# Two-layer convolution block on one core: scattered evictions in every group, sums on VectorE, separate result tiles at the end of the 7x7 stage

## The chip, the core and the metric

The kernel runs on one core of a Trainium2 chip. The metric is the device time of one execution in microseconds; the median of several runs is compared. TensorE (PE) multiplies, VectorE (DVE), ScalarE (ACT) and GpSimd (POOL) do the rest, and SyncE (SP), ACT and POOL issue transfers to 16 DMA engines. All data are 32-bit floats.

## What is computed

The input x has 384 channels of 192 x 192 pixels. Layer 0 normalises over groups of 12 channels, projects to q, k and v, takes the maximum over 2 x 2 pixels, runs a 3 x 3 depthwise convolution, forms channel attention in 8 heads with four top-k softmaxes, and adds the projected result to x. Layer 1, which the change touches, is a depthwise 7 x 7 convolution with residual:

```python
w_sym = (weight + rot90(weight, 1) + rot90(weight, 2) + rot90(weight, 3)) * 0.25
x = x + dwconv(groupnorm(x), w_sym, stride=1, pad=3)     # 384 channels, 7 x 7 each
```

## The kernel before

Layer 0 fills the first 2100 us or so and isn't touched. It leaves the new x in device memory as `sd`, cut into an 8 x 8 raster of pixels (64 partitions, each with a coarse image), and the 7 x 7 filters as matrices in `wt`.

The 7x7 stage turns each channel into matmuls. The contraction runs over the pixels of a window and over some marker rows for the borders (126 partitions); the output is 128 partitions, which are places within 8 x 8 cells and row halves, by 288 columns (6 tiles of 24 cells, two strips each). The loop `for n in range(steps)` has 48 steps of `CB` = 8 channels. Each step works in four quarters, `q` = 0 to 3, of two channels: 16 matmuls into one PSUM tile `pc` (there are four, of two banks each), then one eviction into `apart`, which multiplies by the reciprocal deviation `rb` of the channel. Two steps make a group of `CO` = 16 channels, so there are 24 groups (numbers 0 to 23) and one `apart` tile for each.

Around the matmuls these things happen:

- **Loads, two steps ahead.** `load_w` (line 1702, on SP) brings the weights `w` into one of three buffers. `load_main` (line 1711, on POOL) brings the pixels `mains` into 64 partitions of one of three buffers.
- **Copies.** `below` fills the other partitions of `mains` from those that were loaded. POOL copies one part (lines 1864 and 1868), ACT another, each in two instructions. On ACT the first copy follows the eviction of q = 0 and the second that of q = 1.
- **Sums into the weights.** `middle(n + 1)` (line 1769) adds the diagonal for the residual, from `mids`, to the weights of the next step, four channels per instruction. From step 1 on it runs on POOL, after POOL's copies.
- **Evictions.** ACT takes q = 0, 1 and 2 (line 1981), DVE q = 3 (line 1979). In all groups but the last they write rows of 48 elements. In the last group (`dense`) the matmul reads its columns in another order, and the eviction writes single elements 32 words apart, so that what a transpose reads lies together.
- **Transposes.** `swapped` (line 1914) turns 32 x 32 blocks of `apart` into rows of the image in a tile `res`, in six instructions per group. It is a generator: the loop calls it once after each eviction, so group g's transposes run in the two steps after the group. There are two `res` buffers.
- **Stores.** `stored` (line 1889) writes a group with eight transfers on SP. They are put into SP's queue at the start of the second step after the transposes began, behind that step's weight load. For group 22 they are issued after its last transpose. For group 23 they are issued after every second transpose, half on SP and half on ACT.

`keep` holds an instruction at its place in the order in which the program is written. Each engine works in order, and so does each queue: a weight load on SP behind eight stores is issued after them.

Of the kernel before, what the change touches and what calls it, by code (L numbers as in the profile page):

```python
# [8 lines left out]
F32 = mybir.dt.float32  # L9
# [4 lines left out]
P = 128  # L14
# [4 lines left out]
HW = 192  # L19
# [40 lines left out]
TR = 32  # L60
NT = HW // TR
ED = 8
NJ = HW // ED
JP = NJ + 1
STRIPS = NT * JP
PITCH = 160
# [5 lines left out]
Q = 32  # L72
RQ = Q // ED
WIN = 2 * ED
GP = 3 * ED - 3
ONE = (WIN - 1) * ED
ROWS = 6
# [13 lines left out]
CO = 16  # L91
# [4 lines left out]
def conv_preact_d2(  # L96
# [17 lines left out]
    nc = tc.nc  # L114
# [198 lines left out]
    keep = tc.keep_in_program_order  # L313
    with tc.tile_pool(name="stp", bufs=1) as stp, tc.tile_pool(name="xsp", bufs=5) as xsp:
# [77 lines left out]
        mids = stp.tile([P, KT + 1], F32, name="mids0")  # L392
# [4 lines left out]
        for b in reversed(range(NB)):  # L397
            if b == NX - 1:
# [7 lines left out]
                for k, i in ((0, 0), (1, 1), (KT, 2)):  # L406
                    ps = total(f"gs_mid0_{k}", 1, terms[i])
# [56 lines left out]
        for b in [*range(NB - 2, NX, -2), NX, *reversed(range(NX))]:  # L464
            n = 2 if b > NX else 1
# [19 lines left out]
        ps = total("gs0_2", 2, [(sel(1, 2), ds[1]), (shared[:, P:], de), (whole, d)])  # L485
# [124 lines left out]
    with ExitStack() as bx:  # L610
# [269 lines left out]
        begun_dw, ready = {}, []  # L880
# [739 lines left out]
    with ExitStack() as ex_:  # L1620
# [135 lines left out]

        half = (ED + 1) * RQ

        def middle(n, add):

            centre = ws[n].rearrange("p b c n -> p b (c n)")
            for i in range(0, CB, 4):
                g = (n * CB + i) // GC
                mid = bass.AP(
                    ws[n].tensor, ws[n].offset + i * ED * ED,
                    [[ws[n].ap[0][0], 3 * Q], [CB * ED * ED + RQ, 2], [ED, 4 * ED], [1, RQ]],
                )
                keep(
                    add(  # L1769
                        mid, mid,  # L1770
                        mids[0 : 3 * Q, g].unsqueeze(2).to_broadcast([3 * Q, 2, 4, ED * RQ]),
                        ALU.add,
                    )
                )
# [33 lines left out]
        along(sb, std1, 0)()  # L1808
        busy(idle[:, 0], 5)
        middles(0)  # L1810
        middle(0, nc.vector.tensor_tensor)
        sumw = const.tile([P, KT], F32, name="sumw")
        with tc.issue_after(settled):
            nc.vector.tensor_reduce(sumw, w7s.rearrange("p t a b -> p t (a b)"), AX.X, ALU.add)
# [64 lines left out]
            for _ in copying:  # L1879
                pass  # L1880

        def stored(n, res, lo=0, hi=NT, queues=(nc.sync,)):

            for i, quad in enumerate((0, 2, 1, 3)):
                h, g = divmod(quad, 2)
                for k in range(2):
                    row = TURNS[h][k] * ED + (1 - g) * RQ + lo * TR
                    keep(
                        queues[i % len(queues)].dma_start(
                            bass.AP(  # L1890
                                out.tensor, out.offset + (n * CO * HW + row) * HW,
                                [[HW * HW, CO], [TR * HW, hi - lo], [1, RQ * HW]],
                            ),
                            res[quad * Q + k : (quad + 1) * Q : 2, lo:hi].rearrange(
                                "p t r n -> p t (r n)"
                            ),
                        )
                    )

        columns = 2 * NJ  # L1900

        groups = C // CO
        ready = []

        def swapped(n, apart):

            last = n == groups - 1
            res = outp.tile([P, NT, RQ, HW], F32, name=f"res{n}", tag="res")
            for k in range(NT):
                src = apart[:, k].rearrange("p c (s j) -> p j (c s)", j=NJ)  # L1910
                if last:
                    src = apart[:, k].rearrange("p c n -> p (c n)").rearrange("p (j n) -> p j n", j=NJ)
                keep(
                    nc.vector.transpose(  # L1914
                        res[:, k].rearrange("p r (j q) -> p j r q", q=ED)[:, :, ::-1], src
                    )
                )
                if last and k % 2:
                    stored(n, res, k - 1, k + 1, (nc.sync, nc.scalar))
                yield  # L1920
            if n == groups - 2:
                stored(n, res)
            elif not last:
                ready.append(lambda: stored(n, res))

        for lo, hi, copy in ((0, 2, nc.gpsimd), (2, 5, nc.gpsimd), (5, CB, nc.vector)):
            whole(below(0, copy.tensor_copy, *LOWER[0], slice(lo, hi)))
# [5 lines left out]
        for n in range(steps):  # L1933
# [5 lines left out]
            if n + 1 < steps:  # L1939
                for copy, cs in ((nc.gpsimd, slice(0, CB)),) if n else (  # L1940
                    (nc.gpsimd, slice(0, CB // 2)), (nc.vector, slice(CB // 2, CB))
                ):
                    whole(below(n + 1, copy.tensor_copy, *LOWER[0], cs))
                middle(n + 1, nc.gpsimd.tensor_tensor)
            w, main = ws.pop(n), mains.pop(n)
            if n % 2 == 0:
                apart = outp.tile([P, NT, CO, columns], F32, name=f"apart{n}", tag="apart")
            order = [[JP, NT], [PITCH, 2]]
            dense = n // 2 == groups - 1
            if dense:  # L1950
                order.reverse()
            for q in range(CB // 2):
                ps = pc.tile([P, 2, 512], F32, name=f"pc{n}_{q}", tag="pc")
                for k in range(2):
                    i = 2 * q + k
                    for j in range(2):
                        for h in range(2):
                            keep(
                                nc.tensor.matmul(  # L1959
                                    ps[h * 2 * Q : (h + 1) * 2 * Q, k, 0 : 2 * NT * NJ],  # L1960
                                    w[0 : ONE + ROWS, j, i],
                                    bass.AP(
                                        main.tensor, main.offset + i * RUN + 2 * h * PITCH + j,
                                        [[main.ap[0][0], ONE + ROWS], *order, [1, NJ]],
                                    ),
                                    start=(j == 0), stop=(j == 1), skip_group_check=True,
                                )
                            )
                c = n * CB + 2 * q
                o = n % 2 * CB + 2 * q  # L1970
                src = ps[:, :, 0 : 2 * NT * NJ].rearrange("p k (t n) -> p k t n", t=NT)
                dst = apart[:, :, o : o + 2].rearrange("p t k n -> p k t n")
                if dense:
                    src = ps[:, :, 0 : 2 * NT * NJ].rearrange("p k (s n) -> p k s n", s=2)
                    dst = apart.rearrange("p t c n -> p (t c n)").rearrange(
                        "p (n c s) -> p c s n", c=CO, s=2
                    )[:, o : o + 2]
                if q == 3:
                    keep(nc.vector.tensor_scalar_mul(dst, src, rb[:, c : c + 1]))
                else:  # L1980
                    keep(nc.scalar.mul(dst, src, rb[:, c : c + 1]))  # L1981
                next(swapping, None)
                if q == 0 and n + 1 < steps:
                    lower = below(n + 1, nc.scalar.copy, *LOWER[1])
                next(lower, None)
                if q == 1 and n in later:
                    dgs = [diagonal(v, later[n]) for v in (std1, rstd1)]
            if n in later:
# [69 lines left out]
```

## Time and profile before

| | |
|---|---|
| Time, median of 3 runs | 2581.61 us (2578.67 to 2583.24) |
| Profiled execution | 2587.33 us |
| its span | 2585.6 us |
| granted TensorE clock, mean | 0.976 |
| busy shares of the span: PE, DVE, ACT, POOL | 91%, 81%, 51%, 51% |
| 7x7 stage, first to last matmul | 2117.1 to 2556.4 us |
| from last matmul to the end | 29 us |

The profile is one execution; its times count from the start of the span. A row of a group of instructions gives the line in the code, the engine, the operation, what is written and read with its shape, the count, the busy time and mean duration in ns, and after the bar the idle time of the engine just before these instructions with what ended it. A wait for several things is put down to the last that came. A DMA share of 1 means that all 16 DMA engines had a packet in work all the time.

### The profile page before, as it was taken

What the parts mean: (1) busy time and instruction counts of PE and PEld (TensorE: products, weight loads), DVE (VectorE), ACT (ScalarE), POOL (GpSimd) and SP (SyncE); (2) the same over time, 40 slices, a digit from 0 to 9 for tenths busy, and PEclk for the clock granted to TensorE, in tenths of its full rate; (3) what the DMA queues carried; (4) which work ended last, traced back from release to release, by engine and by line L of the source; (5) the groups of instructions that cost most, each with busy time, mean ns of one, the idle gap of its engine ahead of it and who ended that gap; (6) DMA issues with size and microseconds to landing.
All of it is one profiled execution on the core that took longest, in us unless ns stands there. A gap on an engine that the chain in (4) does not pass through costs nothing.

```text
span 2585.6 us, 29955 instructions
## 1 busy us (share of the span) xinstructions
PE 2350.5 (91%) x9655; PEld 1436.8 (56%) x9655; DVE 2098.3 (81%) x2875; ACT 1314.0 (51%) x2424; POOL 1306.6 (51%) x1329
## 2 busy tenths in 40 slices
PE   0298999999999999999989999999999959998995
PEld 0144565555556666665555666666666745565553
DVE  7986688888888887878879999999888958777775
ACT  0031576666667677677521323222322457776774
POOL 1013688888887767766522211211211367767672
PEclk9998999999999999999999999999999979999997
DMA  9995254453553323233343866765764598999997
GB/s 377 404 222 126 71 117 120 106 144 96 118 137 75 97 64 102 58 82 82 80 142 103 240 215 193 259 228 189 245 249 153 207 272 295 334 323 327 331 335 220
DMA packets 439386, 487.14 MB, mean 188 GB/s; under 512 B 291149, under 2 KB 369197, under 8 KB 434749
## 3 DMA queue, kind: packets, MB, share of 16 engines
q1 hardware_dynamic: 407558, 339.17, 43.5%
q0 software_dynamic: 28032, 141.97, 17.1%
q10 hardware_dynamic: 3639, 4.09, 0.6%
q8 instruction: 77, 1.26, 0.2%
q14 instruction: 80, 0.66, 0.1%
HBM read 309.18 MB, written 147.47 MB: 177 GB/s over the span
## 4 chain that ended last, share of the span: by engine, by line
PE 72%; DMA 13%; DVE 9%; ACT 2%; POOL 1%; issue 1%; SPq 1%; ACTq 0%; DVEq 0%; POOLq 0%
PE pv L568 20%; PE bank_b L1040 10%; PE bank_y L1040 7%; PE bank_d L1040 6%; PE bank_c L1040 6%; PE bank_x L1040 6%; PE pc L1959 6%; DMA w<-wt 5%; PE pr L1474 4%; PE po L1450 3%; DVE st L342 3%; DMA out_dram<-res 3%; DMA xs<-in_x_dram 2%; DMA mains<-sd 2%; PE grams L802 2%
## 5 line engine op out<-in xcount | busy, mean ns | idle before, releaser
L568 PE MATMUL pv<-xv,wq 128*128 128x384 f32 x1512 | 495.2, 488 | 10.7 <-DVE rows L574 6.0
L1959 PE MATMUL pc<-mains,w 126*64 126x288 f32 x3072 | 410.8, 420 | 41.1 <-POOL w L1769 25.2
L568 PEld LDWEIGHTS pv<-xv,wq 128*128 128x128 f32 x1512 | 288.5, 191 | 208.8 <-DVE rows L574 6.6
L1541 POOL DMA_DIRECT2D sd<-sx x180 | 135.1, 755 | 529.2 <-DVE sx L1505 517.9
L903 POOL TENSOR_TENSOR qk<-qk,more 128x384 f32<-128x384 f32 x290 | 310.0, 1073 | 142.9 <-ACT more L902 132.8
L1959 PEld LDWEIGHTS pc<-mains,w 126*64 126x64 f32 x3072 | 245.3, 137 | 205.5 <-POOL w L1769 39.6
L1914 DVE STREAM_TRANSPOSE res<-apart 128x768 f32<-128x768 f32 x144 | 282.6, 2011 | 78.1 <-DMA w<-wt 41.3
L601 DVE SCALAR_TENSOR_TENSOR vb<-rows,wd,vb 128x576 f32<-128x576 f32 x360 | 293.6, 817 | 10.7
L903 POOL TENSOR_TENSOR qk<-qk,rows 128x384 f32<-128x384 f32 x216 | 230.2, 1070 | 97.2 <-ACT rows L902 90.2
L935 DVE SCALAR_TENSOR_TENSOR bank_r<-ring,wd,bank_r 128x384 f32<-128x384 f32 x383 | 236.4, 617 | 6.8
L1040 PE MATMUL bank_b<-rows,more 128*128 128x384 f32 x528 | 219.8, 498 | 9.2 <-ACT bank_c L1140 9.0
L1505 DVE TENSOR_TENSOR sx<-xr,y 128x576 f32<-128x576 f32 x180 | 204.1, 1175 | 18.1 <-ACT y L1482 15.2
L1119 DVE TENSOR_TENSOR rows<-bank_c,rows 128x384 f32<-128x384 f32 x132 | 73.2, 554 | 137.9 <-PE bank_c L1040 76.4
L574 DVE TENSOR_REDUCE rows<-pv 128x192 f32<-128x768 f32 x144 | 137.6, 956 | 44.1 <-PE pv L568 44.0
L902 ACT ACTIVATE more<-ring,wd 128x384 f32<-128x384 f32 x290 | 170.3, 609 | 0.0
L1525 ACT ACTIVATE wq<-sx,negmid 128x1152 f32<-128x1152 f32 x96 | 120.6, 1256 | 96.6 <-DVE sx L1505 94.3
L1981 ACT ACTIVATE apart<-pc,rb 128x576 f32<-128x576 f32 x144 | 110.2, 765 | 99.4 <-PE pc L1959 61.3
L1040 PE MATMUL bank_x<-xq,wq 128*128 128x384 f32 x378 | 154.7, 491 | 1.0 <-ACT bank_b L1092 1.0
L1040 PE MATMUL bank_y<-xq,wq 128*128 128x384 f32 x378 | 155.0, 492 | 0.0
L1457 ACT ACTIVATE gl<-po 128x288 f32<-128x288 f32 x96 | 39.5, 411 | 222.5 <-PE po L1450 222.5
L1864 POOL COPY mains<-mains 32x2560 f32<-32x2560 f32 (+3 forms) x49 | 110.0, 2246 | 75.9 <-DMA mains<-sd 74.8
L1474 PE MATMUL pr<-gl,wp 128*128 128x288 f32 x576 | 142.6, 406 | 0.0
(343 smaller groups left out, 4474.4 us busy)
## 6 DMA issues: line engine op xcount, KB each, us to landing
mains<-sd POOLq DMA_DIRECT2D x46, 1312.0 KB, 10.3
out_dram<-res SPq DMA_DIRECT2D x184, 288.0 KB
xr<-in_x_dram SPq DMA_DIRECT2D x45, 1152.0 KB
xq<-in_x_dram SPq DMA_DIRECT2D x21, 2304.0 KB
xv<-in_x_dram SPq DMA_DIRECT2D x126, 384.0 KB
sd<-sx POOLq DMA_DIRECT2D x132, 320.0 KB, 7.8
xs<-in_x_dram SPq DMA_DIRECT2D x24, 1536.0 KB
w<-wt SPq DMA_DIRECT2D x47, 504.0 KB
```

The costliest lines, as they stand in the source:

```text
L568: nc.tensor.matmul(ps[:, u, 0 : RB * HW], wq[:, kt, o : o + P], xb[:, u, kt, :], start=(kt == 0), stop=(kt == KT - 1),)
L574: nc.vector.tensor_reduce(rows[ct][:, 1 + t0 : 1 + t0 + UT, 1 : PS + 1], ps[:, :, 0 : RB * HW].rearrange("p u (a w b) -> p u w a b", a=2, ...
L601: pin(nc.vector.scalar_tensor_tensor(dst, src, w, dst, ALU.mult, ALU.add))
L902: keep(nc.scalar.mul(part.rearrange("p (h w) -> p h w", w=PS), src, w))
L903: keep(nc.gpsimd.tensor_tensor(flat, flat, part, ALU.add))
L935: nc.vector.scalar_tensor_tensor(into, src, w, before, ALU.mult, ALU.add)
L1040: nc.tensor.matmul(ps[:, 0:HN], lhs, rhs, start=start, stop=True, skip_group_check=True)
L1474: nc.tensor.matmul(ps[:, 0:H], wp[:, ct, ot * P : (ot + 1) * P], gl[:, ct, h * H : (h + 1) * H], start=(ct == 0), stop=(ct == KT - 1),)
L1505: nc.vector.tensor_tensor(bass.AP(flat.tensor, flat.offset + 1 + (a * ED + e) * STRIPS, [flat.ap[0], [JP, NT], [1, NJ], [2 * STRIPS, ED // ...
L1541: engine.dma_start(sdv[r + a, cs, RQ - e : ED - e, o : o + n], bass.AP(flat.tensor, flat.offset + 1 + (a * ED + e) * STRIPS - (e > 0), [fl ...
L1914: nc.vector.transpose(res[:, k].rearrange("p r (j q) -> p j r q", q=ED)[:, :, ::-1], src)
L1959: nc.tensor.matmul(ps[h * 2 * Q : (h + 1) * 2 * Q, k, 0 : 2 * NT * NJ], w[0 : ONE + ROWS, j, i], bass.AP(main.tensor, main.offset + i * RU ...
```

## The change

- `middle` always runs on VectorE. In the loop it is called at q = 3, just ahead of the eviction of q = 3, instead of after POOL's copies.
- All groups use the column order and the scattered evictions of the former last group, and all transposes read dense blocks. `apart` is laid out for that.
- Evictions with even q are on ACT and those with odd q on VectorE: two each per step.
- ACT makes both of its copies after the eviction of q = 0.
- `places` names the tiles of a group's results. Groups 0 to 21 have one `res` tile as before. Group 22 has half of a `res` tile and the space of `edges`; group 23 has a third of one `res` tile, the space of `mids`, and a third of another. `edges` and `mids` are no longer needed by then.
- Group 22 is stored in two halves, each as soon as its three transposes are issued; group 23 in three parts, as before on SP and ACT.

```diff
-                middle(n + 1, nc.gpsimd.tensor_tensor)
...
+        def places(n):
+
+            def spare(t, k):
+                flat = bass.AP(t.tensor, t.offset, [t.ap[0], [1, k * RQ * HW]])
+                return flat.rearrange("p (t r n) -> p t r n", t=k, n=HW)
+
+            def own(i):
+                return outp.tile([P, NT, RQ, HW], F32, name=f"res{n}_{i}", tag="res")
+
+            if n < groups - 2:
+                return [own(0)]
+            if n == groups - 2:
+                return [own(0)[:, 0 : NT // 2], spare(edges, NT // 2)]
+            return [own(0)[:, 0:2], spare(mids, 2), own(1)[:, 0:2]]
+
         def swapped(n, apart):
 
-            last = n == groups - 1
-            res = outp.tile([P, NT, RQ, HW], F32, name=f"res{n}", tag="res")
-            for k in range(NT):
-                src = apart[:, k].rearrange("p c (s j) -> p j (c s)", j=NJ)
-                if last:
-                    src = apart[:, k].rearrange("p c n -> p (c n)").rearrange("p (j n) -> p j n", j=NJ)
-                keep(
-                    nc.vector.transpose(
-                        res[:, k].rearrange("p r (j q) -> p j r q", q=ED)[:, :, ::-1], src
+            k = 0
+            for res in places(n):
+                for i in range(res.shape[1]):
+                    keep(
+                        nc.vector.transpose(
+                            res[:, i].rearrange("p r (j q) -> p j r q", q=ED)[:, :, ::-1],
+                            apart[:, k + i],
+                        )
                     )
-                )
-                if last and k % 2:
-                    stored(n, res, k - 1, k + 1, (nc.sync, nc.scalar))
+                    if i + 1 < res.shape[1]:
+                        yield
+                if n < groups - 2:
+                    ready.append(lambda: stored(n, res))
+                else:
+                    stored(n, res, k, (nc.sync, nc.scalar) if n == groups - 1 else (nc.sync,))
                 yield
-            if n == groups - 2:
-                stored(n, res)
-            elif not last:
-                ready.append(lambda: stored(n, res))
+                k += res.shape[1]
...
-                apart = outp.tile([P, NT, CO, columns], F32, name=f"apart{n}", tag="apart")
-            order = [[JP, NT], [PITCH, 2]]
-            dense = n // 2 == groups - 1
-            if dense:
-                order.reverse()
+                apart = outp.tile([P, NT, NJ, 2 * CO], F32, name=f"apart{n}", tag="apart")
...
-                                        [[main.ap[0][0], ONE + ROWS], *order, [1, NJ]],
+                                        [[main.ap[0][0], ONE + ROWS], [PITCH, 2], [JP, NT], [1, NJ]],
...
-                src = ps[:, :, 0 : 2 * NT * NJ].rearrange("p k (t n) -> p k t n", t=NT)
-                dst = apart[:, :, o : o + 2].rearrange("p t k n -> p k t n")
-                if dense:
-                    src = ps[:, :, 0 : 2 * NT * NJ].rearrange("p k (s n) -> p k s n", s=2)
-                    dst = apart.rearrange("p t c n -> p (t c n)").rearrange(
-                        "p (n c s) -> p c s n", c=CO, s=2
-                    )[:, o : o + 2]
-                if q == 3:
+                src = ps[:, :, 0 : 2 * NT * NJ].rearrange("p k (s n) -> p k s n", s=2)
+                dst = apart.rearrange("p t j (c s) -> p c s (t j)", s=2)[:, o : o + 2]
+                if q == 3 and n + 1 < steps:
+                    middle(n + 1)
+                if q % 2:
                     keep(nc.vector.tensor_scalar_mul(dst, src, rb[:, c : c + 1]))
...
                 if q == 0 and n + 1 < steps:
                     lower = below(n + 1, nc.scalar.copy, *LOWER[1])
-                next(lower, None)
+                    next(lower)
+                    next(lower)
```

More of the change, by code (lines that the diff above doesn't have):

```diff
@@ L1757, in conv_preact_d2, with middle @@
         half = (ED + 1) * RQ
-        def middle(n, add):
+        def middle(n):
             centre = ws[n].rearrange("p b c n -> p b (c n)")
@@ L1768, in middle @@
                 keep(
-                    add(
+                    nc.vector.tensor_tensor(
                         mid, mid,
@@ L1810, in conv_preact_d2 @@
         middles(0)
-        middle(0, nc.vector.tensor_tensor)
+        middle(0)
         sumw = const.tile([P, KT], F32, name="sumw")
@@ L1880, in whole, with stored @@
                 pass
-        def stored(n, res, lo=0, hi=NT, queues=(nc.sync,)):
+        def stored(n, res, lo=0, queues=(nc.sync,)):
             for i, quad in enumerate((0, 2, 1, 3)):
@@ L1891, in stored @@
                                 out.tensor, out.offset + (n * CO * HW + row) * HW,
-                                [[HW * HW, CO], [TR * HW, hi - lo], [1, RQ * HW]],
+                                [[HW * HW, CO], [TR * HW, res.shape[1]], [1, RQ * HW]],
                             ),
-                            res[quad * Q + k : (quad + 1) * Q : 2, lo:hi].rearrange(
-                                "p t r n -> p t (r n)"
-                            ),
+                            res[quad * Q + k : (quad + 1) * Q : 2].rearrange("p t r n -> p t (r n)"),
@@ L1897, in stored @@
                         )
                     )
-        columns = 2 * NJ
         groups = C // CO
         ready = []
-        def swapped(n, apart):
-            last = n == groups - 1
-            res = outp.tile([P, NT, RQ, HW], F32, name=f"res{n}", tag="res")
-            for k in range(NT):
-                src = apart[:, k].rearrange("p c (s j) -> p j (c s)", j=NJ)
-                if last:
-                    src = apart[:, k].rearrange("p c n -> p (c n)").rearrange("p (j n) -> p j n", j=NJ)
-                keep(
-                    nc.vector.transpose(
-                        res[:, k].rearrange("p r (j q) -> p j r q", q=ED)[:, :, ::-1], src
-                    )
-                )
-                if last and k % 2:
-                    stored(n, res, k - 1, k + 1, (nc.sync, nc.scalar))
+        def places(n):
[9 more added lines that the diff above has]
+            return [own(0)[:, 0:2], spare(mids, 2), own(1)[:, 0:2]]
```

## The prediction

> **What bounds the kernel now.** All edits lie in the 7x7 stage, so I read first the busy time by stretch: the stage without its start and end (2162 to 2538 us), and the end (2556 to 2586 us). Columns: length; busy time (instructions) of PE, PE weight load, DVE, ACT, POOL; granted clock; DMA share; GB/s.
>
> ```profile
> 2162.00:2538.00 376.00, 350.00 (x2625) 209.54 (x2626) 277.68 (x167) 275.97 (x206) 261.35 (x205) 0.97 0.97 331
> 2386.00:2394.00 8.00, 8.00 (x44) 4.11 (x46) 5.96 (x4) 3.82 (x4) 6.92 (x6) 0.67 0.97 324
> 2266.00:2274.00 8.00, 8.00 (x68) 4.55 (x66) 6.85 (x4) 5.71 (x5) 6.39 (x5) 1.00 0.80 237
> 2556.00:2586.00 30.00, 0.39 (x2) 0.00 (x0) 6.69 (x7) 0.00 (x0) 0.00 (x0) 0.54 0.60 157
> ```
>
> DVE, ACT and POOL work about 70 to 74% of the stage, PE 93%, and the DMA engines 97%. One step (8 channels) moves 504 KB of weights, 1312 KB of pixels and, on average, 1152 KB of results: 3.04 MB, at 331 GB/s 9.2 us. From the timeline, 40 steps (last VectorE eviction at 2170.96 to that at 2538.76) take 367.8 us: 9.2 us each. Undisturbed, a step takes 8.4 us (PE from 2413.26 to 2421.67). So the transfers set the pace. The missing 0.8 us per step comes in lumps: two or three groups run free, then the chain shows this.
>
> ```profile
> 2369.44 15.60 DMA w<-wt
> 2385.08 0.10 issue
> 2385.18 0.73 POOL w L1769
> 2385.95 27.10 PE pc L1959 x193
> ```
>
> Weights issued behind eight stores land late, POOL adds the sums, PE starts 3.6 us late; afterwards its clock is 0.67 for some microseconds, and only then has the DMA a little air (0.75 to 0.88 in such slices). The waits say the same; the columns are total us, times, longest.
>
> ```profile
> DVE res L1914 <- DMA w<-wt: 41.3, 14, 4.4
> DVE res L1914 <- DMA out_dram<-res: 29.5, 7, 11.8
> PE pc L1959 <- POOL w L1769: 25.2, 13, 3.6
> POOL w L1769 <- DMA w<-wt: 12.3, 9, 2.2
> ```
>
> The second part is the end: the last PE matmul is at 2556.4, the span ends at 2585.6. The timeline from the last group's evictions (first two rows, step 46) on:
>
> ```profile
> 2544.81 1.35 ACT L1981 ACTIVATE apart<-pc,rb 128x576 f32<-128x576 f32 x1
> 2548.57 1.20 DVE L1979 TENSOR_SCALAR apart<-pc,rb 128x576 f32<-128x576 f32 x1
> 2557.70 1.84 DVE L1914 STREAM_TRANSPOSE res<-apart 128x768 f32<-128x768 f32 x2
> 2571.31 1.84 DVE L1914 STREAM_TRANSPOSE res<-apart 128x768 f32<-128x768 f32 x2 [11.78 <-DMA out_dram<-res]
> 2577.82 1.84 DVE L1914 STREAM_TRANSPOSE res<-apart 128x768 f32<-128x768 f32 x2 [4.67 <-DMA out_dram<-res]
> ```
>
> The transposes of one tile wait for the stores of its earlier parts: 16.45 us in all, though the data don't meet. The DMA share is 0.60 here.
>
> **The change, part by part.** The last group of before already has the scattered evictions and dense transposes, so their prices stand in the trace. For the rest, the stage's groups:
>
>
> ```profile
> L1914 DVE STREAM_TRANSPOSE res<-apart 128x768 f32<-128x768 f32 x144 | 282.6, 2011 | 78.1 <-DMA w<-wt 41.3 <-DMA out_dram<-res 29.5 <-ACT mains L1864 6.9
> L1981 ACT ACTIVATE apart<-pc,rb 128x576 f32<-128x576 f32 x144 | 110.2, 765 | 99.4 <-PE pc L1959 61.3 <-issue 35.7
> L1979 DVE TENSOR_SCALAR apart<-pc,rb 128x576 f32<-128x576 f32 x48 | 39.3, 819 | 54.6 <-PE pc L1959 54.6
> L1769 POOL TENSOR_TENSOR w<-w,mids 96x256 f32<-96x256 f32 x94 | 66.7, 727 | 15.3 <-DMA w<-wt 12.3
> L1864 POOL COPY mains<-mains 32x1280 f32<-32x1280 f32 x1 | 1.9, 1895 | 1.0 <-DMA mains<-sd 1.0
> ```
>
> *Load per step.* DVE before: 3 transposes x 2.01 + 1 eviction x 0.82 = 6.85 us. After: 3 x 0.92 (1.84 for two, above) + 2 evictions x 1.20 + 2 sums x 0.42 (the two that DVE did before the stage, 415 and 422 ns) = 6.0. ACT: 3 x 0.74 + copies 2.32 + 2.19 = 6.7 before, 2 x 1.31 + 4.51 = 7.1 after. POOL: 0.52 + 2.31 + 2.19 + 2 x 0.73 = 6.5 before, 5.0 after. All stay under the 8.4 us of PE. As busy time this saves DVE about 40 us and POOL 68, and none of it is on the path while the transfers set the pace: it buys nothing by itself. The matmuls only read their columns in another order, as the last group does already at the same speed.
>
> [...]
>
> *ACT order.* ACT now runs eviction q0, then both copies, without q1 between them. The next step's matmuls wait for the copies: 0.74 + 2.32 + 0.74 + 2.20 = 6.0 becomes 1.3 + 2.32 + 2.20 = 5.8. The free step of 8.4 us ends with this chain (PE waits 0.2 us for ACT's copy), so it can fall to about 8.2; and where pixels land late, ACT is 0.7 us quicker. Both are gains of compute that the transfers can take back.
>
> *Sums to DVE.* They stood on POOL behind its copies of the next pixels and ahead of its next pixel DMA; a late weight transfer held that DMA back (issued at 2386.54, where PE was free for it near 2382.3). Now that DMA goes out up to 4 us earlier after a stall. After a late landing PE waits for 2 x 0.42 instead of 2 x 0.73 us: 0.6 us x 8 stalls = 5 us. But on DVE the sums stand behind the eviction q1 and two transposes, and in a group's first step the first transpose waits for the stores of two groups before. Call T the time from the step's start to that transpose. The second sum ends at max(T + 0.95, 4.3) + 1.2 + 1.9 + 0.84, about T + 5.0, or 8.3 if T is under 3.35. From the DVE timeline, T over 21 groups is 0.7 to 7.6, mean 3.5. Where T is largest the weights were later still (10 us and more after the step's start), so the new wait hides behind the old; over the other groups the excess sums to 3 to 4 us of PE. Behind a sum that waits stand eviction q3 and the next transposes; PE needs that PSUM buffer only 6.4 us into the next step, and results leave two steps later, so nothing else is late.
>
> [...] The row agrees that there is contention (POOL's half copy beside DVE's copies took 1895 ns, half of the usual 2310 is 1155). If POOL lost all of 2 x 0.42, its step would be 5.9 us instead of 5.0, still under the 6.5 of before. I take nothing on the path.
>
> Stage, summed: -5 (shorter add) - 5 (ACT order, 30 free steps x 0.18) + 4 (sums behind late stores), about -6 of compute, of which the saturated transfers give half: **-3 us**. Bounds: the DMA share of 0.97 leaves 3% of 376, so -12 at best; +5 if the excess of T counts in full and nothing is gained.
>
> *End.* With own tiles no transpose waits for its neighbours' stores: six of 0.92 from 2557.7, done at 2563.3. Group 22 is now stored in halves, the first in step 46 and the second at about 6.5 us into step 47 (2555), where before all eight stores (2.36 MB) were issued only after the last slow transpose at 2555.6. Group 23's stores, four on SP and four on ACT per pair, at 0.6 to 0.8 us an issue: SP first works off the second half until about 2560, then 12 x 0.7 = 8.4 us, to 2568.5. Each store also waits in the program for a DMA eight issues before it, so a pair follows the landing of the last one, 2.2 to 2.5 us (the last two in the chain of before): three pairs from 2560 end issuing at 2568 as well. Landing 2.5, end 0.9: 2571.5 against 2585.6, **-14 us**. By bytes, 3.5 MB from 2555 at 331 GB/s end at 2566 plus landing, so the DMA doesn't forbid it. Bounds: -16 (issues at 0.6) and -9 (issues at 1.35 us as in the stage, eleven on SP's way). The new third tile takes the buffer of group 22's first half, landed well before 2561: no wait of weight.
>
> **Sum.** -14 - 3 = -17. The profiled execution took 2587.33 us, its span 2585.6 (1.7 around it), so 2570.3 for it; it stands 5.7 above the median of the runs, 2581.61, from which I forecast 2564.6.
>
> **Rivals.**
> (1) *The stage gains as well.* [...] For it: the dips to 0.75 come only after a PE stall. Against it: the stage moves the same bytes, and most slices are full.
> (2) *The end doesn't give what it should.* If the remaining transfers or the issue queues set the end, -9 or less there and +3 in the stage: 2575.6. For it: stores took 1.35 us an issue in the stage. Against it: a share of 0.60 at the end.
> (3) *Slower: the sums wait behind the transposes on DVE.* One mechanism: in each group's first step, stores landing late hold the transpose, the eviction q1 and so the next step's weights. Price: T - 3.35 per group, 21 groups. It decides against the end's 14 us when the mean excess passes 0.67 us, that is T about 4.0 in every group, with nothing given back by the transfers. Ten of 21 groups have T at 4.0 or above now. At T = 4.5 everywhere it costs 24 and the time is 2592. Against it: most of these late groups wait for their weights longer anyway, and a delayed PE issues fewer transfers, which brings T down.
>
> **How the numbers follow.** Forecast 0.60 (own range 2558 to 2573), rival 1 0.17, rival 2 0.13, rival 3 0.10. Single runs of before spread by 0.2%, 5.2 us, which is about what can be told from no change. Faster: 0.60 + 0.17 + half of rival 2 = 0.83; same: the other half and a little of rival 3, 0.08; slower 0.09. The range takes the forecast, rival 1 to -12 and -16, rival 2 to -9 and +5: 2553 to 2578.
>
> **What would show it.** Right: dense transposes near 0.92 us and DVE evictions near 1.20 in every group; the mean step between 8.9 and 9.2 us at a DMA share of 0.96 or more; no transpose after the last matmul waiting for a DMA; last matmul to end about 15 us instead of 29. Wrong: PE waiting mostly for the sums on DVE while weights have landed (rival 3); a step of 8.6 (rival 1); stores after the last matmul that queue behind one another past 20 us (rival 2).

## The result, and the profile after

The changed kernel takes 2594.64 us (median of 16 runs, 2588.39 to 2604.25), the kernel before, run beside it, 2584.64 us (16 runs, 2578.67 to 2599.57). The ratio is 1.0035, with a 95% interval of 1.0021 to 1.0049: slower by 0.35%, some 9 us, where 17 us less were forecast.

The two profiled executions (2587.33 us before, 2597.32 us after) can be cut at the first and the last matmul of the 7x7 stage:

| | before | after | forecast |
|---|---|---|---|
| first to last matmul of the stage | 439.3 us (2117.1 to 2556.4) | 451.7 us (2115.6 to 2567.3) | -3 us |
| last matmul to the end | 29.2 us | 28.2 us | -14 us |

So the stage lost 12.4 us and the end gained 1.0. Both accounts failed, for different reasons. The busy time by stretch of the kernel after, with the columns of the prediction (length; PE, PE weight load, DVE, ACT, POOL busy; clock; DMA share; GB/s):

```profile
2162.00:2538.00 376.00, 335.72 (x2540) 248.09 (x2536) 231.54 (x277) 273.49 (x158) 193.63 (x118) 0.94 0.93 318
2386.00:2394.00 8.00, 7.13 (x34) 3.52 (x36) 4.90 (x4) 2.89 (x3) 4.18 (x2) 0.58 0.99 354
2394.00:2402.00 8.00, 8.00 (x70) 4.57 (x68) 4.98 (x7) 6.33 (x5) 3.45 (x3) 1.00 0.53 156
2562.00:2570.00 8.00, 5.28 (x43) 3.76 (x38) 4.74 (x6) 2.03 (x2) 0.00 (x0) 1.00 0.14 35
2567.00:2595.50 28.50, 0.28 (x2) 0.00 (x0) 6.58 (x7) 0.00 (x0) 0.00 (x0) 0.56 0.59 145
```

VectorE lost 46 us of work and GpSimd 68, about as counted, and yet PE was busy 14 us less in the same stretch. The transfers, which were to set the pace at a share of 0.97, fell to 0.93: they are no longer full. The second and third row show one such place: after a stall of PE its clock is 0.58 for a stretch, the transfers catch up, and in the next 8 us they run half empty (0.53), since the next pixel transfer is issued only at 2398.55, after PE has finished its slow step. In the kernel before, whose stall ended at nearly the same time, the share in these 8 us was 0.85. The fourth row is a hole at the end, 8 us with the DMA engines at 0.14.

The groups of the same execution show that the single prices were right: transposes 0.95 us, evictions 1.22 on VectorE and 1.27 on ScalarE (forecast 0.92, 1.20, 1.31).

```profile
L1922 DVE STREAM_TRANSPOSE res<-apart 128x768 f32<-128x768 f32 x139 | 129.3, 954 | 35.0 <-DMA w<-wt 15.7 <-ACT mains L1868 8.4 <-DMA out_dram<-edges 6.8
L1983 ACT ACTIVATE apart<-pc,rb 128x576 f32<-128x576 f32 x96 | 121.6, 1266 | 93.1 <-PE pc L1964 63.4 <-issue 28.6
L1981 DVE TENSOR_SCALAR apart<-pc,rb 128x576 f32<-128x576 f32 x96 | 117.5, 1224 | 109.0 <-PE pc L1964 108.9
```

The waits of the stage (total us, times, longest) say what PE stood for:

```profile
POOL mains L1711 <- PE pc L1964: 80.2, 25, 7.9
PE pc L1964 <- DVE w L1769: 43.7, 14, 6.5
DVE w L1769 <- DMA w<-wt: 31.0, 8, 5.5
```

PE waited 25.2 us for the sums before, 43.7 now, and up to 6.5 us at a time instead of 3.6. The third line tells whose fault it is: in eight of the nine stalls of 3 us or more the sums themselves waited for weights, 31.0 us in all. In these they don't stand behind transposes, as rival 3 had it. Only in the longest (6.5 us) do they: VectorE's first transpose ran at 2193.11, and the sums, behind it, an eviction and two more transposes, at 2196.73. How late weights come about is in the chain of waits ahead of one stall, and in the timeline of GpSimd beside it (start, duration). L1711 issues a pixel transfer, two steps ahead; L1864 copies the pixels of one step ahead, so it reads what the L1711 before the last one brought:

```profile
2357.26 8.16 DMA out_dram<-res
...
2365.49 19.73 DMA w<-wt
2385.22 0.02 issue
2385.24 2.90 DVE w L1769 x2
2388.14 0.04 issue
2388.19 2.18 PE pc L1964 x7
```

```profile
2365.15 0.50 POOL L1711 DMA_DIRECT2D mains<-sd  x1 [2.81 <-ACT mains L1868]
2373.25 0.50 POOL L1711 DMA_DIRECT2D mains<-sd  x1 [3.14 <-PE pc L1964]
2380.63 2.31 POOL L1864 COPY mains<-mains 32x2560 f32<-32x2560 f32 x1 [6.88 <-DMA mains<-sd]
2385.02 0.50 POOL L1711 DMA_DIRECT2D mains<-sd  x1
2398.55 0.50 POOL L1711 DMA_DIRECT2D mains<-sd  x1 [8.37 <-ACT apart L1983]
```

The time from issue to landing of the transfer issued at 2373.25 (KB, us), then the issue and the landing time of its counterpart in the kernel before:

```profile
mains<-sd POOLq DMA_DIRECT2D x1, 1312.0 KB, 11.5
```

```profile
2374.48 0.52 POOL L1711 DMA_DIRECT2D mains<-sd  x1 [0.84 <-ACT mains L1868]
mains<-sd POOLq DMA_DIRECT2D x1, 1312.0 KB, 10.3
```

The weights (504 KB, SyncE's queue, behind eight stores) were issued at 2365.49 and landed at 2385.22. The pixels of the next step (1312 KB, GpSimd's queue) were issued 7.8 us later, at 2373.25, and landed 11.5 us after that, 0.4 us before the weights: 2.6 times the bytes overtook them. Why the larger transfer landed first, no run here shows.

This overtaking is not what the change brought, though. In the chain of before that the prediction shows, the weights went out at 2369.44 and landed at 2385.04; the pixels of the next step went out 5.0 us after them and landed 0.3 us before them. That transfer stands ahead of the sums in both programs. What the moved sums set free is the pixel transfer after it, the one at 2385.02. Before, GpSimd never issued it earlier than 1.4 us after the sums began, and so never before the weights had landed. Now it went out 1.8 to 3.8 us ahead of the sums at three of the nine stalls; at the other six it went out between 0.2 us ahead of them and 1.0 us behind. This is the transfer that the prediction counted as a gain when it "goes out up to 4 us earlier".

That GpSimd's freedom costs time is shown by the second experiment below. How it does so stays open. In the chain of the changed kernel the weights were in flight for 17.2 to 19.7 us at six of eight stalls, in that of the kernel before for 16.5 us at most; but in the stall shown the freed transfer left only as they landed.

The end has the next two views, the timeline of VectorE and of SyncE's queue (issues of stores):

```profile
2568.59 1.84 DVE L1922 STREAM_TRANSPOSE res<-apart 128x768 f32<-128x768 f32 x2
2570.35 1.80 DVE L1922 STREAM_TRANSPOSE mids<-apart 128x768 f32<-128x768 f32 x2
2578.94 1.84 DVE L1922 STREAM_TRANSPOSE res<-apart 128x768 f32<-128x768 f32 x2 [6.79 <-DMA out_dram<-edges]
```

```profile
2549.68 26.34 SPq L1889 DMA_DIRECT2D out_dram<-res  x16
2576.12 8.78 SPq L1889 DMA_DIRECT2D out_dram<-edges  x8
2585.00 2.49 SPq L1889 DMA_DIRECT2D out_dram<-res  x4
2587.59 2.49 SPq L1889 DMA_DIRECT2D out_dram<-mids  x4
2590.18 2.49 SPq L1889 DMA_DIRECT2D out_dram<-res  x4
```

The own tiles did what they should for the transposes: one wait of 6.79 us is left of two with 16.45. But SyncE takes 26 us over sixteen stores: within the first half of group 22 it issues nothing from 2562.5 to 2572.8. The second half (in the tile called edges), transposed by 2565.5, is issued only from 2576.1. That the last pair of transposes waited at all belongs to it: its buffer was that of the first half, whose stores were now late.

What SyncE waits for stands in the built program of this kernel. In it, eight DMA semaphores go round over the stores in the order in which they were planned, over both queues, and a store waits for the one that had its semaphore before it. Here are four stores in this order, of group 22's first half (SP, res22) and of group 23 (ACT), with the semaphore of each and the value it waits for:

```
SP  res22  DMAHW1 [2640]
ACT mids   DMAHW2 [2640]
SP  res22  DMAHW3 [2640]
ACT mids   DMAHW4 [2640]
```

Semaphore 3 reaches 2640 only with ScalarE's first store of group 23. So a store of group 22 that was ready at 2562 waited for a store of a group that PE hadn't finished. In the trace, SyncE's stores wait 15.7 us from 2540 on for earlier stores to land, up to 10.3 us at a time; in the kernel before it is 3.6 us, up to 3.0.

### The profile page after: what moved, and what is told of

Its sections match the earlier page's. It is cut to its first block, busy times and chain, and to the rows that moved or that the text cites. A ratio compares the mean times of both kernels' runs of the same rounds, so it can differ in the third digit from the quotient of the medians.

```text
span 2595.5 us, 29970 instructions
## 1 busy us (share of the span) xinstructions
PE 2344.8 (90%) x9655; PEld 1491.0 (57%) x9655; DVE 2058.2 (79%) x3017; ACT 1320.8 (51%) x2376; POOL 1240.5 (48%) x1235
## 4 chain that ended last, share of the span: by engine, by line
PE 74%; DMA 14%; DVE 6%; POOL 2%; SPq 1%; issue 1%; ACT 1%; ACTq 0%; DVEq 0%; POOLq 0%
PE pv L568 19%; PE bank_b L1040 10%; PE bank_y L1040 7%; DMA w<-wt 7%; PE pc L1964 7%; PE bank_d L1040 6%; PE bank_c L1040 6%; PE bank_x L1040 6%; PE pr L1474 4%; PE po L1450 3%; DMA out_dram<-res 3%; DMA xs<-in_x_dram 2%; PE grams L802 2%; DVE st L342 1%; PE bank_b L714 1%
## 5 line engine op out<-in xcount | busy, mean ns | idle before, releaser
L1964 PE MATMUL pc<-mains,w 126*64 126x288 f32 x3072 | 406.4, 421 | 58.5 <-DVE w L1769 43.7
L1964 PEld LDWEIGHTS pc<-mains,w 126*64 126x64 f32 x3072 | 300.4, 141 | 163.4 <-POOL mains L1868 31.7
L1981 DVE TENSOR_SCALAR apart<-pc,rb 128x576 f32<-128x576 f32 x96 | 117.5, 1224 | 109.0 <-PE pc L1964 108.9
L1983 ACT ACTIVATE apart<-pc,rb 128x576 f32<-128x576 f32 x96 | 121.6, 1266 | 93.1 <-PE pc L1964 63.4
L1922 DVE STREAM_TRANSPOSE res<-apart 128x768 f32<-128x768 f32 x139 | 129.3, 954 | 35.0 <-DMA w<-wt 15.7
L1864 POOL COPY mains<-mains 32x2560 f32<-32x2560 f32 (+3 forms) x49 | 111.3, 2271 | 86.3 <-DMA mains<-sd 86.3
```

Source lines behind the costliest of these rows:

```text
L1922: nc.vector.transpose(res[:, i].rearrange("p r (j q) -> p j r q", q=ED)[:, :, ::-1], apart[:, k + i],)
L1964: nc.tensor.matmul(ps[h * 2 * Q : (h + 1) * 2 * Q, k, 0 : 2 * NT * NJ], w[0 : ONE + ROWS, j, i], bass.AP(main.tensor, main.offset + i * RU ...
```

## The experiments

Each kernel is profiled once; stage and end are of that execution. Executions of one kernel differ by more than most of the effects (2571.0 to 2598.1 us for the kernel before beside the first four experiments), so where stage and ratio disagree the ratio (against the kernel before run beside it, with its 95% interval) decides.

| kernel | median us | ratio | stage | end |
|---|---|---|---|---|
| before | 2584.6 | 1 | 439.3 | 29.2 |
| after | 2594.6 | 1.0035 (1.0021 to 1.0049) | 451.7 | 28.2 |
| sums back on GpSimd | 2582.7 | 0.9984 (0.9970 to 0.9999) | 435.7 | 28.6 |
| GpSimd held by the weights | 2578.7 | 0.9987 (0.9969 to 1.0005) | 430.9 | 28.3 |
| last group on one queue | 2586.0 | 0.9996 (0.9981 to 1.0012) | 451.4 | 21.5 |
| slower free steps | 2587.9 | 1.0018 (1.0001 to 1.0035) | 438.9 | 28.4 |
| held, one queue | 2577.4 | 0.9967 (0.9952 to 0.9983) | 443.5 | 21.8 |
| weights on GpSimd's queue | 2575.4 | 0.9961 (0.9942 to 0.9980) | 428.9 | 28.7 |
| weights on GpSimd's queue, last group on one queue | 2568.6 | 0.9934 (0.9910 to 0.9957) | 433.0 | 21.8 |
| held, one queue, slower free steps | 2577.5 | 0.9975 (0.9957 to 0.9994) | 445.6 | 21.6 |
| before, sums on VectorE | 2593.2 | 1.0033 (1.0017 to 1.0050) | 444.4 | 27.5 |
| before, weights on GpSimd's queue | 2584.8 | 1.0001 (0.9987 to 1.0015) | 441.1 | 28.7 |
| before, weights on GpSimd's queue, sums on VectorE | 2583.9 | 1.0005 (0.9993 to 1.0017) | 440.6 | 28.1 |
| weights and sums on GpSimd | 2646.6 | 1.0253 (1.0229 to 1.0277) | 506.5 | 29.0 |

**Sums back on GpSimd.** In the changed kernel, the sums go where they were; everything else stays.

```diff
+                middle(n + 1, nc.gpsimd.tensor_tensor)
             w, main = ws.pop(n), mains.pop(n)
...
-                if q == 3 and n + 1 < steps:
-                    middle(n + 1)
```

> The changed kernel, with the sums into the weights back on GpSimd, behind its copies and ahead of its next pixel transfer; all else as changed. Theory A (the moved sums lengthen the stage: pixel transfers are no longer held back behind late weights and take their bandwidth, and the sums themselves are slowed beside GpSimd's copies): the stage, 451.7 us from first to last matmul after the change and 439.3 before, goes back to 440 or less, total 10 to 14 us under the changed kernel, at or a little under the kernel before. Theory B (quicker free steps, 8.0 instead of 8.4 us, only make the stalls on late weights longer and the clock drops deeper; the place of the sums does not matter): the stage stays at 449 to 453.

Measured: 2582.7 us, 0.5% under the changed kernel (1.0035 to 0.9984, intervals apart), stage 435.7 us. The stretch from 2162 to 2538 us:

```profile
2162.00:2538.00 376.00, 342.44 (x2628) 206.64 (x2626) 203.96 (x207) 284.94 (x164) 261.16 (x205) 0.96 0.97 334
```

The loss of the stage came with the move of the sums, and without it the new evictions, transposes and ScalarE's new order cost nothing. PE waits 33.4 us for sums here, more than the 25.2 us of before, and yet no time is lost: the transfers are as full as before (0.97). So a longer wait of PE was not a loss by itself; the changed kernel's emptier transfers (0.93) were.

**GpSimd held by the weights.** The sums stay on VectorE. GpSimd only reads one column of the weights (24 elements) before it goes on to the next pixel transfer.

```diff
+        seen = wide.tile([P, 1], F32, name="seen")
...
                     whole(below(n + 1, copy.tensor_copy, *LOWER[0], cs))
+                keep(nc.gpsimd.tensor_copy(seen[3 * Q : ONE], ws[n + 1][3 * Q : ONE, 0, 0, 0:1]))
```

> The changed kernel, where GpSimd after its copies reads one column of 24 rows of the next weights that the sums do not touch, so that its next pixel transfer waits for the weights to land as before, while the sums stay on VectorE. If theory A holds through the early pixel transfers: the stage falls to 443 or less, total 8 us or more under the changed kernel, and the DMA share of the stage rises from 0.93 towards 0.97. If theory A holds only through slow sums beside GpSimd's copies, or if theory B holds: no change of the stage beyond 3 us.

Measured: 2578.7 us, stage 430.9 us; the interval of its ratio lies below that of the changed kernel. The stretch and the waits:

```profile
2162.00:2538.00 376.00, 343.07 (x2670) 275.62 (x2668) 241.30 (x293) 289.74 (x167) 213.54 (x165) 0.97 0.97 337
```

```profile
PE pc L1966 <- DVE w L1770: 25.0, 13, 3.6
PE pc L1966 <- DMA out_dram<-res: 7.7, 1, 7.7
POOL seen L1955 <- DMA w<-wt: 16.1, 8, 3.9
```

This run decides between two readings of the one before: with the sums on VectorE and the hold restored, the kernel is as fast as with the sums on GpSimd (0.9987 and 0.9984). So the sums are harmless on VectorE; what cost was the loss of the hold that GpSimd had with them. GpSimd waits 16.1 us for weights, and its next pixel transfer never goes out before they have landed. The sums' own waits for weights fall from 31.0 to 14.9 us, PE's waits from 43.7 to 32.7 us: the second line, put down to a store, is one more stall in which PE waited for the sums (let go at 2197.32, it ran four matmuls and waited 0.70 us more for them, until 2199.33). The transfers are full again (0.97).

The hold delays two things, GpSimd's pixel transfer and the copies behind it, and the copies slow the sums when they meet (one sum took up to 2.55 us instead of 0.41; see the last section). That is the smaller part: at PE's waits for sums of over 0.5 us, the pairs of sums took 15.9 us in all in the changed kernel and 13.0 here. The rest goes with weights that are in time more often. Which of the effects of a later pixel transfer brings that about, no run separates.

**Last group on one queue.** SyncE alone stores group 23.

```diff
-                    stored(n, res, k, (nc.sync, nc.scalar) if n == groups - 1 else (nc.sync,))
+                    stored(n, res, k)
```

> The changed kernel, with all stores of the last group on SyncE's queue instead of half on ScalarE's. Theory C (the stores share eight semaphores in the planner's order over both queues, so group 22's stores on SyncE wait for group 23's on ScalarE, which wait for the last transposes): group 22's stores are done before the last matmul, and the 28.2 us from last matmul to the end fall to 15 to 19, total 10 to 13 us under the changed kernel; the stage stays at 451. Theory D (issues and bytes of the last stores set the end): one queue with 24 issues of 0.6 us takes longer, 28 us or more.

Measured: stage as in the changed kernel (451.4 us), end 21.5 us, 2586.0 us (1.0035 to 0.9996, intervals apart). SyncE's issues:

```profile
2544.66 14.56 SPq L1889 DMA_DIRECT2D out_dram<-res  x14
2560.57 5.05 SPq L1889 DMA_DIRECT2D out_dram<-edges  x8
2565.72 5.05 SPq L1889 DMA_DIRECT2D out_dram<-res  x8
2570.87 5.04 SPq L1889 DMA_DIRECT2D out_dram<-mids  x8
2576.01 5.03 SPq L1889 DMA_DIRECT2D out_dram<-res  x8
```

The hole is gone with the second queue: the sixteen stores before it take SyncE 16.4 us (2542.84 to 2559.22) instead of 26.3, and the second half of group 22 goes out from 2560.57 instead of 2576.12. One queue is faster here than two that wait for each other (an end of 21.5 us against 28.2). The gain in the end is 6.7 us, less than expected, because 32 issues at 0.63 us now follow one another.

**Slower free steps.** One more matmul of 288 columns per step, into a PSUM tile that is overwritten afterwards. The trace has it as two records, 0.75 us together, so it is 36 us in 48 steps, more than the 0.4 us each that were reckoned with.

```diff
                 ps = pc.tile([P, 2, 512], F32, name=f"pc{n}_{q}", tag="pc")
+                if q == 2:
+                    busy(ps[:, 0], 1)
```

> The changed kernel with one further matmul of 128x128 by 288 columns per step, which is overwritten: it slows the free step by about 0.4 us, to the 8.4 us of before. Theory B: the stage gets no longer or shorter, 440 to 452, with shorter stalls. Theory A alone: the step time adds where the transfers do not hide it, 451 to 460.

Measured: 2587.9 us. The profiled stage is 12.8 us shorter with 36 us more work in it, and its stretch has PE at a clock of 0.99:

```profile
2162.00:2538.00 376.00, 364.42 (x2738) 208.80 (x2735) 247.21 (x295) 287.39 (x166) 203.74 (x123) 0.99 0.98 334
```

PE waits for the sums 10.0 us in all here, against 43.7: here PE ran ahead less, met fewer late weights and kept its clock (0.99, where the changed kernel has 0.94). By the medians the gain is 0.2%, and its interval overlaps that of the changed kernel; so this is support, not proof. What is sure is that 48 more matmuls cost nothing against the changed kernel.

**Held, one queue.** The second and third edit together.

> The changed kernel with two edits together: GpSimd held until the weights have landed (as in the run where a small GpSimd copy reads them), and the last group stored on SyncE's queue alone. If the stage and the end are separate accounts, they add: stage near 431 us, end near 21.5 us, so some 7 us under the held kernel, 2572 us, 0.5% under the kernel before. If a stage that is 13 us shorter only leaves more stores for the end to carry out, the end is 26 us or longer and the time stays at 2577 to 2580 us.

Measured: 2577.4 us, the time of the second case with the end of the first (21.8 us). By the ratios the second edit adds 0.2% to the first (0.9987 to 0.9967), 5 us of the 7, but these intervals overlap. The profiled execution was one of the slowest of its kernel (2586.6 us), so its stage of 443.5 us says little. It shows that the hold doesn't take the stalls away: PE waited 35.9 us for the sums in it, up to 7.1 us at a time.

**Weights on GpSimd's queue.** In the changed kernel the weights are issued in the queue of the pixels, ahead of them, and no longer behind the stores.

```diff
-                ws[n + 2] = load_w(n + 2)
+                ws[n + 2] = load_w(n + 2, nc.gpsimd)
                 mains[n + 2] = load_main(n + 2, nc.gpsimd)
```

> The changed kernel, the weight transfers of the 7x7 stage issued by GpSimd just ahead of the pixel transfer instead of by SyncE behind the stores. Theory: weights are late because they stand behind eight stores in SyncE's queue; then TensorE's waits for the sums fall from 43.7 us to under 10 us, the stage from 451.7 to 415 to 430 us, and the time to 2561 to 2574 us. Rival: they are late because the transfers as a whole are behind, in whichever queue they stand; then the waits for sums stay above 30 us, or waits for pixels take their place, the stage stays at 445 to 455 us, and the time is 2588 to 2598 us.

Measured: 2575.4 us, stage 428.9 us. The stretch, then PE's waits in it:

```profile
2162.00:2538.00 376.00, 346.40 (x2697) 260.51 (x2695) 287.33 (x296) 291.49 (x168) 240.51 (x164) 1.00 0.99 338
```

```profile
PE pc L1964 <- DVE w L1769: 16.8, 14, 1.8
PE pc L1964 <- POOL mains L1868: 12.5, 13, 1.1
```

No stall is longer than 1.8 us, the mean clock is 1.00, the transfers are at 0.99. The weights, issued 0.8 us ahead of the pixels, land after 8.7 us and the pixels after 11.4 us (medians of this stretch), and VectorE never waits for weights. The waits didn't fall under the 10 us that the theory gave, but from 43.7 to 16.8; the stage is that of the theory, and the time, 1.4 us above its range, is far from its rival's. The edit does two things: the weights stand ahead of the pixels, and no longer behind the stores. Which of the two helps isn't divided here.

**The same, with the last group on one queue.**

> The changed kernel with the weights issued by GpSimd ahead of the pixel transfer and the last group stored on SyncE's queue alone. Weights on GpSimd's queue gave a stage of 428.9 us and an end of 28.6 us, 2575.4 us in all. If the end takes what the same edit gave elsewhere (28.2 to 21.5 us), the time is 2568 to 2570 us, 0.6% under the kernel before. If, as with the held kernel (2578.7 without, 2577.4 with this edit), the gain is lost again elsewhere, it is 2574 to 2576 us.

Measured: 2568.6 us, within the first case; the end is 21.8 us. This version is 0.66% faster than the kernel before and 1.0% faster than the changed one (0.9934 / 1.0035). It still has all of the change in it.

**Held, one queue, slower free steps.** All three edits.

> The changed kernel with GpSimd held until the weights have landed, the last group on SyncE's queue alone, and one more matmul of 288 columns in each step (idle work of 0.46 us). Each of the two stage edits by itself gave 13 to 21 us in the stage. If both work by the same cause (fewer stalls on late weights, with their low clock and the empty transfers after them), the second adds nothing: stage 428 to 436 us, within 4 us of the kernel without the extra matmul. If they work by different causes, they add: stage 415 to 423 us, 8 us or more under it. If neither helps and TensorE is the bound once GpSimd is held, the 46 extra matmuls cost their 21 us in part: stage 437 us or more.

Measured: 2577.5 us, the same as without the extra matmul (2577.4). The stage of 445.6 us is not the 428 to 436 expected, but its companion's was 443.5 in its own profiled execution; beside that one it is within 4 us. The two edits don't add, which fits that they act on the same stalls.

**Before, sums on VectorE.** The kernel before, with this one part of the change.

```diff
-                middle(n + 1, nc.gpsimd.tensor_tensor)
...
+                if q == 3 and n + 1 < steps:
+                    middle(n + 1, nc.vector.tensor_tensor)
                 if q == 3:
```

> The kernel before with one part of the change alone: the sums into the weights on VectorE instead of GpSimd, evictions and transposes as before. Theory that letting GpSimd go on without the weights, and so send its pixel transfers early, is what costs: the stage grows from 439 to 447 to 453 us, the time to 2592 to 2599 us. Rival, that only the quicker free steps of the new evictions cost: stage 437 to 443 us, 2582 to 2588 us. Third, that the sums wait behind VectorE's transposes of two us: TensorE waits for sums whose weights had landed 3 us or more before, in over half of the groups, and VectorE's wait for weights is small.

Measured: 2593.2 us (1.0033), the whole loss of the change from one of its parts, as the first theory has it. But the third theory has its marks as well. VectorE's timeline at one stall, PE beginning at 2399.51:

```profile
2392.83 6.01 DVE L1914 STREAM_TRANSPOSE res<-apart 128x768 f32<-128x768 f32 x3 [3.06 <-DMA w<-wt]
2398.78 0.71 DVE L1769 TENSOR_TENSOR w<-w,mids 96x256 f32<-96x256 f32 x2
```

Here three transposes of two us, themselves held until 2392.8, stand ahead of the sums, and VectorE waited for the weights in three cases only (7.3 us). With long transposes rival 3's mechanism is real. The loss in this kernel can't be divided between the two, since it was not run with the hold as well. In the changed kernel, where the transposes are short and VectorE waited for weights in eight of nine long stalls, rival 3 is left with the one stall told above.

**Before, weights on GpSimd's queue.** The kernel before with the edit that issues the weights ahead of the pixels.

> The kernel before with one edit: the weights of the 7x7 stage issued by GpSimd ahead of the pixel transfer, not by SyncE behind the stores. If late weights in SyncE's queue are what both kernels lose to, and the change only meets them more often, this kernel gains as well: stage 428 to 433 us, 2574 to 2579 us, the same as the changed kernel with this edit. If the changed kernel suffers from something that only it has, this one gains little: 2582 to 2586 us.

Measured: 2584.8 us, no gain. **The same with the sums on VectorE:**

> The kernel before with the weights issued by GpSimd and the sums on VectorE; its own evictions, and transposes of 2.01 us. If the place of the sums alone makes the difference once the weights are in time, the stage is 428 to 434 us and the time 2574 to 2580 us. If VectorE also needs the short transposes, because sums and evictions stand behind up to three of two us each, the stage is 438 to 446 us and the time 2583 to 2592 us, with TensorE waiting for sums 25 us or more.

Measured: 2583.9 us, no gain either. PE's waits in the stretch from 2162 to 2538 us, first of the former, then of the latter:

```profile
PE pc L1959 <- POOL w L1769: 28.3, 16, 5.0
PE pc L1959 <- ACT mains L1868: 0.4, 2, 0.2
```

```profile
PE pc L1958 <- ACT mains L1868: 16.4, 24, 1.8
PE pc L1958 <- DVE w L1769: 9.6, 10, 1.6
```

With the weights in time, the kernel before waits for GpSimd's sums (which stand behind its copies of 4.5 us), and with those moved it waits for ScalarE's copies, which have an eviction between them. So the other parts of the change do pay, once the weights are in time: 2583.9 becomes 2575.4 (1.0005 to 0.9961, intervals apart) with short transposes, even evictions and ScalarE's new order. Which of these three it is wasn't divided further. (The ends of both are alike, 28.1 and 28.7 us, so the tiles of the last two groups have no part in it.)

**Weights and sums on GpSimd.** The changed kernel with the sums back on GpSimd and the weights on its queue as well.

> The changed kernel with the weights issued by GpSimd and the sums put back on GpSimd: evictions and transposes of the change remain. Weights on GpSimd's queue gave the changed kernel 2575.4 us and the kernel before 2584.8. If the place of the sums makes that difference (on GpSimd they stand behind its copies of 4.5 us and TensorE waits for them in nearly every step), this one is near the second: 2582 to 2588 us, TensorE's waits for sums 25 us or more. If the dense transposes and scattered evictions make it, it is near the first: 2573 to 2578 us.

Measured: 2646.6 us, which neither theory had. It doesn't answer the question, for the edit moved something else. PE's waits:

```profile
PE pc L1965 <- ACT apart L1982: 57.0, 16, 5.4
PE pc L1965 <- POOL w L1769: 4.5, 2, 4.0
```

In the built program the four PSUM buffers, named by their first bank, come in another order (tiles q = 0 to 3 of two steps):

```
changed kernel                4 0 2 6   4 0 2 6
weights and sums on GpSimd    4 2 4 4   6 0 2 6
```

In every second step q = 3 takes the buffer of q = 2, and must wait for the eviction of that tile, which on ScalarE stands behind two copies. The planner chose this order; why stays open. In no other kernel of the table does PE wait longer than 1.4 us for an eviction in this stretch.

## Why the prediction was wrong

*Single prices and load per step.* Right: 0.95, 1.22 and 1.27 us, and all engines stay under the pace of PE (VectorE 232, ScalarE 273 and GpSimd 194 us busy in the 376 us of the stretch, PE 336).

*ACT order.* Its direction was right and its size too small: the free step fell from 8.4 to about 7.9 us (VectorE's evictions at 2356.86, 2364.62 and 2372.72), against 8.2 forecast. The step from there, "the saturated transfers give half", took the transfers for elastic. At the 331 GB/s of the kernel before, 3.04 MB take 9.2 us, not 7.9; the time that PE gains per step comes back as a longer stall. Before, six steps took some 55 us from stall to stall (9.15 us each), after, four took some 39 (9.8 each). What the quicker step costs by itself isn't shown: with the sums back on GpSimd it costs nothing, and the extra matmul per step, which is free, only points to a part of it.

*Sums to DVE.* This is the step that failed in the stage. "Now that DMA goes out up to 4 us earlier after a stall" was put among the gains, with no question of what GpSimd's wait had been good for, though the weights that PE waits for were in flight at that moment. Measured, the restored hold is worth 0.5% (1.0035 to 0.9987), 12 us, more than the whole loss. The +4 us for sums behind late stores, and rival 3 with it, looked for the danger on VectorE; PE's wait did grow by 18.5 us, but mostly for weights.

*Contention of POOL and VectorE.* The prediction let GpSimd pay for it, found it covered and took "nothing on the path". It is VectorE that pays; in the stall shown, two sums of together 0.8 us took 2.90 us while PE waited.

```profile
L1769 DVE TENSOR_TENSOR w<-w,mids 96x256 f32<-96x256 f32 x96 | 44.0, 497 | 31.0 <-DMA w<-wt 31.0
```

At 497 ns instead of 410 the 96 sums lost 8 us, nearly all in four stalls, where PE waited for them. That takes away the 5 us of the shorter add: at PE's waits of over 0.5 us, 11 in both kernels, the pairs of sums took 15.9 us in all, and 15.6 on GpSimd before.

*End.* The transposes went as forecast up to the last pair; the stores didn't, and this is the step that failed in the end. "Each store also waits in the program for a DMA eight issues before it" was right, but I counted these eight in each queue by itself. They are counted over both, in planned order, and so a store of group 22 stood behind one of group 23. "SP first works off the second half until about 2560" became 2584.9. Rival 2 had named the issue queues as what sets the end, at -9 us; with one queue they give -7.7 (29.2 to 21.5). "No wait of weight" for the buffer of the third tile was wrong for the same reason: 6.79 us.

*The range.* Its upper end, 2578, was made of small terms (+5 in the stage, -9 at the end). A loss of the stage from a GpSimd that no longer waits for weights was not among the cases, and the only slower case had another mechanism.

## What to carry to other kernels

Where transfers are saturated (a share of 0.97 here), an engine's wait may be worth keeping: GpSimd's wait for the weights was worth 0.5%. Before a wait is taken away, list what will be issued earlier and what is in flight then. Try the urgent transfer ahead of the large one in the same queue: here that was worth 0.7% in the changed kernel and nothing in the kernel before, where the next limit stood behind it. Where two queues share semaphores that go round, read in the built program which store waits for which: here the second queue delayed the first, and the end took 28.2 us with two queues and 21.5 with one. A change that gains nothing may still be a gain once the next limit is gone: here it lost 0.35% alone and was part of a version 0.66% faster.

## What the runs showed of the hardware

- A transfer of 1312 KB issued on GpSimd's queue 7.8 us after one of 504 KB on SyncE's queue, which stood behind eight stores, landed 0.4 us before it.
- When the sums on VectorE met GpSimd's copies, VectorE lost: one of two sums took up to 2.55 us instead of 0.41, while GpSimd's copies took 2.33 and 2.39 us instead of 2.31 and 2.18. With the weights on GpSimd's queue the sums took 1.02 us on average, as their group shows; there most of it was hidden (PE waited 16.8 us for sums in all).

```profile
L1769 DVE TENSOR_TENSOR w<-w,mids 96x256 f32<-96x256 f32 x84 | 82.3, 1018 | 0.0
```

  What holds VectorE so long when the two meet, no run here shows.
- After a stall of 5.3 us PE's clock was 0.58 over 8 us, and the DMA share fell to 0.53 in the 8 us after those. After one of 3.6 us in the kernel before, the clock was 0.67 and the share 0.85. In these two cases the longer stall of PE cost the transfers more, later.
